# A 17-tap convolution by nested products, woven into a graph network: a bank reassigned, a zero tap dropped, and three asks moved

## The chip, the cores and the metric

The kernel runs on one core of a Trainium2 chip. A core has a matrix engine (TensorE, called PE in the profile, with its weight loads listed as PEld), a vector engine (VectorE, DVE), an activation engine (ScalarE, ACT), a general engine (GpSimd, POOL) and a queue engine (SyncE, SP). Each runs its own stream of instructions in the order in which it was written, and they wait for one another by semaphores. TensorE writes its results to PSUM, a small memory of eight banks of 2 KB per partition; everything else works in SBUF, and transfers to and from the device's main memory are issued on queues by SyncE, GpSimd or ScalarE. The metric is the time of one execution in microseconds (us) of device time, as a median over runs.

## The reference

The input `x` has 32 batches of 512 nodes with 256 channels, and `adj` is one 512 x 512 mask of zeros and ones per batch. All is fp32. Cut to what matters, it computes

```python
h0 = relu(layernorm(x))                              # per node
c  = relu(bn1(conv1x1(h0.T)))
c  = bn2(conv1d(c, conv2_w, 17 taps, pad 8))
x_conv = relu(c + h0.T).T
s  = h0 @ w_se.T + b_se                              # 3 values per node
A  = exp(-dist(s, s)) * adj
x_nmp  = A @ relu(h0 @ w_msg.T + b_msg)
gi = concat(x_conv, x_nmp) @ w_ih.T + b_ih           # GRU cell
gh = h0 @ w_hh.T + b_hh
r, z = sigmoid(gi_r + gh_r), sigmoid(gi_z + gh_z)
out = x + (1 - z) * tanh(gi_n + r * gh_n) + z * h0
```

## The kernel before

**Five streams of work.** The kernel is written as five Python generators: `rows` (normalised rows of the first batches, and the 1x1 convolution `conv1` of all), `begins` (normalise and turn a batch, and store it to `hd` in main memory), `graphs` (messages, exponents, mask, gather), `conv` (the 17-tap convolution) and `gates` (the GRU cell, and the store of the result). A loop at the end of the kernel (`while streams`) takes one step at a time of the stream that is most behind its share. A number `now` stands for TensorE's time and is advanced by every matmul written; a step can say that it is not ready before a certain `now`. Work of the other engines is written by `fill`, which empties a list `LATER` of things due by now (`later(t, f)`), evacuates finished convolution results, and writes operand sums for VectorE (`background`). All of that is decided when the program is built: on the chip there are five fixed instruction streams.

**`settle()`** writes everything that is in `LATER` at once, whatever its due time. It is called in `reset` of the gates, in `graph`, at the second result of each five in the convolution's sums (`summed`), and at the end of each half of the gates.

**The convolution.** The 928 columns of all batches (29 units of 18 outputs each, 32 batches) are cut into seven groups at `STARTS`. Its 17 taps are padded to 18 = 3 x 3 x 2, the first of them zero (line 262), and worked by two nested levels of a three-tap scheme with five evaluation points each, so that a group takes 25 products (`n` from 0 to 24, in the order `ORDER` of points, outer `j1`, inner `j2`). Each product is itself a two-tap convolution. In group 0 it is written out as 16 matmuls. In groups 1 to 6 it takes 12: the sum of both weights (`w[:, 2]`) times the second half of the operand into bank 0 of the PSUM tile `ps_c`; ScalarE copies bank 0 onto bank 1; then each weight times a difference of operand halves (`xd`, made by `ends` on VectorE) is added to its bank. Weights are loaded again from main memory (`wd`) for each product, and `third_weight` makes the sum of both in group 1. The results of five products are combined by VectorE into `z`, and these into `y` (9 values per column); ScalarE also writes the first `y` of a group by three scaled copies of `z`.

**Evacuation.** When a group's `y` is complete, `EVAC` lists its batches, and `evacuate` writes each (bn2 on ScalarE into `part`, then a store to `cd` by GpSimd). Product `n == 4` of the next group waits until `EVAC` is empty (line 774).

**The exponents.** `kernel_exp` takes four PSUM banks for the four 128 x 512 pieces of a batch's distance matrix: three from the pool `ps_g` and a fourth, `extra`, which from group 1 on is bank 0 of a tile `ps_c`, the same pool of one buffer (`cps`) as the convolution's. `bank_at` is set so that the next product is not written before ScalarE has read that bank (lines 789 and 885).

**Rows.** A batch from the eighth on is turned by a detour through main memory: GpSimd stores its rows to `xd`, SyncE loads them back in blocks into `x_sb` (line 943 by `blocks`), VectorE transposes them into `hT`, GpSimd stores that to `hd` (line 954), and SyncE loads it again where it is wanted: `hT` for `conv1` (line 210), `hTg` for the graph and `hTb` for the gates. `load_row` is followed by a delay of 8 in `now`.

**Gates.** A batch's gates read `hTb`, the convolution's result `xconv` (loaded from `cd` by `load_conv`, line 230, added to `hTb` and put through a relu by `residual`), and the gathered sums `xnb`. A result is stored by GpSimd in four pieces (`store`), and the residual input of the next batch, `res`, is loaded by SyncE (`load_res`) into one of two buffers. Its load has to wait until the store has left the buffer. It is asked at `later(now + 5.0, ...)` behind the store (line 1103).

SyncE's queue holds, in one order, the loads of weights, masks, rows, sums, residuals and convolution results. A load that waits holds up all that stand behind it.

Of the kernel before, what the change touches and what calls it, by code (L numbers as in the profile page):

```python
# [32 lines left out]
U = 29  # L33
Q = 18

STARTS = (0, 116, 251, 386, 522, 657, 792, 928)
NG = len(STARTS) - 1
UG = max(j - i for i, j in zip(STARTS, STARTS[1:]))
PER = (STARTS[-1] - STARTS[1]) / (NG - 1) / U
TURNED = 8  # L40
LEAD = 9


ORDER = (3, 0, 4, 2, 1)
# [4 lines left out]
def kernel(  # L49
# [515 lines left out]
    def weights_again(m):  # L565

        w = new_w()
        k = 2 if m < 50 else 3
        nc.sync.dma_start(w[:, :k], WD[m % 25][:, :k])
        WS.append(w)  # L570
        W_AT.append(now + 7.0)

    thirds = set()

    def third_weight(m):
        if m in thirds:
            return
        thirds.add(m)
        w = WS[m]
        dve.tensor_tensor(w[:, 2], w[:, 0], w[:, 1], op=ALU.add)  # L580
        later(dve.free + 0.4, lambda: nc.gpsimd.dma_start(WD[m % 25][:, 2], w[:, 2]))
        W_AT[m] = dve.free + LAG
# [12 lines left out]
    def summed(g):  # L595

        nonlocal read
        y = None  # L600
        _, nh, nz, _ = sizes(g)

        def columns(name, **more):
            return cv.tile([P, NZ], F32, name=name, **more)[:, :nz]

        def add(dst, a, b, op=ALU.add):
            SUMS.append((sums_at, lambda: dve.tensor_tensor(dst, a, b, op=op)))

        def copy(dst, src, scale):
            SUMS.append((sums_at, lambda: later(  # L610
                dve.free + 0.1, lambda: act.activation(dst, src, AF.Copy, scale=scale)
            )))

        def more(dst, a, k, b, op=ALU.add):
            SUMS.append((
                sums_at, lambda: dve.scalar_tensor_tensor(dst, a, k, b, op0=ALU.mult, op1=op)
            ))

        def both(dst, ps):

            nonlocal bank_at, sums_at
            act.activation(dst.rearrange("p (h n) -> p h n", h=2), ps, AF.Copy)
            bank_at = sums_at = act.free + LAG

        for j1 in ORDER:
            got = yield
            sum_all(read)
            n3 = columns("n", bufs=2)
            both(n3, got)
            got = yield  # L630
            sum_all()
            settle()
            z = cv.tile([P, 3 * NZ], F32, name="z")[:, : 3 * nz].rearrange("p (e n) -> p e n", e=3)
            zends = z[:, 0:3:2, :]
            both(z[:, 0, :], got)
            add(z[:, 0, :], z[:, 0, :], n3)
            got = yield
            both(z[:, 2, :], got)
            more(z[:, 2, :], n3, 4.0, z[:, 2, :])
            got = yield  # L640
            n2 = columns("n", bufs=2)
            both(n2, got)
            got = yield
            n1 = z[:, 1, :]
            both(n1, got)
            add(n2, n1, n2, ALU.subtract)
            more(n1, n1, 2.0, n2, ALU.subtract)
            add(zends, zends, n1[:, None, :].to_broadcast([P, 2, nz]))
            more(z[:, 1, :], n3, 2.0, n2)
            read = summed_to + len(SUMS)  # L650
            if j1 == 3:
                y = cv.tile([P, 9 * NZ], F32, name="y")[:, : 9 * nz].rearrange("p (e f n) -> p e f n", e=3, f=3)
                copy(y[:, :, 0], z, 1.0)
                copy(y[:, :, 1], z, 2.0)
                copy(y[:, :, 2], z, 4.0)
            elif j1 in (0, 4):
                add(y[:, :, j1 // 2], y[:, :, j1 // 2], z)
            else:
                for f in range(3):
                    add(y[:, :, f], y[:, :, f], z, ALU.subtract if (f, j1) == (1, 2) else ALU.add)  # L660
        SUMS.append((sums_at, lambda: EVAC.extend(
            (dve.free + 0.3, y, g, b, o) for b in batches(g) for o in range(ND)
        )))
        yield
# [33 lines left out]
    X2, X_AT, XD = [], [], {}  # L698
    at_product = 0
    wide = in_product = exp_waits = False  # L700
    freed, made, made_at, bank_at = -1, 0, 0.0, 0.0

    def all_operands():
# [28 lines left out]

    def convolution():

        nonlocal at_product, cps, wide, in_product

        def product(ps, *terms, clear=(True, True)):

# [22 lines left out]

        for g in range(NG):
            sums = summed(g)
            next(sums)
            nu, nh, nz, rv = sizes(g)
            if g == 1:
                first_ctx.close()
                cps = ctx.enter_context(tc.tile_pool(name="cps2", bufs=1, space=PSUM))
                ps = cps.tile([P, 2, N], F32, name="ps_c")
                matmul(ps[:, 1, :NH], ident, h1[:, :NH], start=True, stop=True)  # L770
                wide = True
            for n in range(25):
                at_product = m = 25 * g + n
                if n == 4:
                    yield lambda: not EVAC
                while 25 <= len(WS) < min(m + 3, 25 * NG):
                    weights_again(len(WS))
                if m == 24:
                    yield lambda: len(WS) >= 25
                if late is None and len(WS) >= 25:  # L780
                    late_pools()
                yield lambda: len(X2) > m and len(WS) > m
                if 25 <= m + 1 < 50 and W_AT[m + 1] <= now:
                    third_weight(m + 1)
                for k in (m, m + 1):
                    if 25 <= k < len(X2) and k not in XD:
                        XD[k] = ends(X2[k], sizes(k // 25)[3])
                        X_AT[k] = dve.free + LAG
                yield max(X_AT[m], W_AT[m], bank_at if g > 0 else 0.0)
                if exp_waits:  # L790
                    yield lambda: not exp_waits
                    yield bank_at
                if 25 <= m < 50:
                    third_weight(m)
                    yield W_AT[m]
                w, x2 = WS[m], X2[m]
                if g == 0:
                    ps = cps.tile([P, N], F32, name="ps_c")[:, :nz]
                    d0, d1, d2 = (x2[:, 0, :], 0), (x2[:, 1, :], 0), (x2[:, 0, :], 1)
                    product(ps[:, :nh], (0, *d0), (1, *d1))  # L800
                    hand()
                    yield now
                    product(ps[:, nh:], (0, *d1), (1, *d2))
                else:
                    in_product = True
                    ps = cps.tile([P, 2, N], F32, name="ps_c")[:, :, :nh]
                    product(ps[:, 0, :], (2, x2[:, 1, :], 0), clear=(True, False))
                    act.activation(ps[:, 1, :], ps[:, 0, :], AF.Copy)
                    yield act.free + LAG
                    for k in range(2):  # L810
                        product(ps[:, k, :], (k, XD[m][:, k, :], 0), clear=(False, False))
                    del XD[m]
                WS[m] = X2[m] = None
                done = ps if g > 0 else ps.rearrange("p (h n) -> p h n", h=2)
                if g > 0:
                    later(now + 0.3, hand)
                at_product = m + 1
                yield now
                if g > 0:
                    yield lambda: done is None  # L820
            hand()
# [44 lines left out]
    def kernel_exp(at):  # L866

        nonlocal now, bank_at, exp_waits
        exp_waits = False
        if not wide:  # L870
            extra = acc.tile([P, N], F32, name="ps_acc")
        else:
            extra = cps.tile([P, 2, N], F32, name="ps_c")[:, 0, :]
        pss = [extra, bank(), bank(), bank()]
        for c in range(NT):
            k = slice(32 * c, 32 * c + 5)
            nc.tensor.matmul(  # L877
                pss[c], gr.left[k, :], gr.right[k, :], start=True, stop=True,
                tile_position=(32 * c, 0),
            )  # L880
        now += 1.15
        for c in range(NT):
            act.activation(at[:, c, :], pss[c], AF.Exp)
            if c == 0:
                bank_at = act.free + LAG

    def masked(b, at, c):

# [130 lines left out]
    def gates(b):  # L1019
# [73 lines left out]
        def store(y, o, s):  # L1093
# [6 lines left out]
                )  # L1100
            if s.stop == N:
                del XR[b, o]
                later(now + 5.0, lambda: load_res(b + 1, o))

        for o in range(ND):
            r = z = None
# [104 lines left out]
    turn_of = 0  # L1211

    def sum_some():
        if not SUMS or SUMS[0][0] > max(now, dve.free) + 0.1:
            return False
        sum_all(summed_to + 1)
        return True
# [7 lines left out]
    def background():  # L1225
# [9 lines left out]
        if sum_some():  # L1235
            return True
        for m in range(max(25, at_product), min(len(WS), 50)):
            if m not in thirds and W_AT[m] <= now:
                third_weight(m)
                return True  # L1240
        for _ in range(3):
# [177 lines left out]
```

## Time and profile before

| what | value |
|---|---|
| median of 5 runs | 2117.6 us (2111.85 to 2118.55) |
| the profiled execution | 2111.85 us, span 2110.0 us |
| TensorE busy | 2055.1 us (97%) |
| VectorE, ScalarE, GpSimd busy | 1368.8, 814.9, 339.4 us |
| matmul records of `ps_c<-xd,w` and `ps_c<-x,w` | 2400 and 2000 |
| TensorE's waits for `hT<-hd`, for `xconv`, for the exponents | 12.8, 7.4 and 6.7 us |
| SyncE's wait for stores of `out_dram<-res` | 471.3 us in 102 waits |

The profile is of one execution; its own time, 2111.85 us, is the time to hold against its rows, and the median is another matter. An fp32 matmul leaves two records in it, so 2400 records are 1200 matmuls. A record's mean duration is not what a matmul costs, since they overlap; the cost is the distance from one to the next in a run without waits. In the list of waits, a line gives the engine and what it was about to write, what it waited for, the total in us, how often, and the longest. In a timeline, a line gives the start, the length of a run of like instructions, and in brackets how long the engine stood still before it, and for what. A helper records most operations, so that L126 (vector and activation) and L135 (matmuls) are lines of helpers, and tiles tell the work apart.

### The profile page before, as it was taken

How to read it: one execution, taken by the hardware profiler on the slowest of the kernel's cores; microseconds unless marked ns; L12 is line 12 of the kernel's file. 1: busy time of each engine (PE TensorE's matmuls, PEld its weight loads, DVE VectorE, ACT ScalarE, POOL GpSimd, SP SyncE). 2: the span in 40 equal slices, each digit the busy share in tenths (PEclk: the TensorE clock that was granted, in tenths of full speed). 3: DMA queues.
4: the chain of work that ended last, by engine and by line, in shares of the span. 5: the costliest groups of instructions: out<-in, count | busy, mean ns of one | idle time of the engine just before them, and what ended most of it. 6: DMA issues, size and time to landing. Idle time of an engine off the chain costs nothing.

```text
span 2110.0 us, 25907 instructions
## 1 busy us (share of the span) xinstructions
PE 2055.1 (97%) x8764; PEld 1260.1 (60%) x8764; DVE 1368.8 (65%) x2448; ACT 814.9 (39%) x1431; POOL 339.4 (16%) x582
## 2 busy tenths in 40 slices
PE   9999899999999999999999999999999989999998
PEld 5887665656566655666556665456665556654444
DVE  6887677877677485786567772667763846654323
ACT  5544453344433344333354333434333432224121
POOL 2001121121211112111121110211111111012111
PEclk9999999999999999999999999999999999999999
DMA  7456798676777777766586766775767455734342
GB/s 287 161 185 193 242 261 225 174 230 181 216 188 201 205 193 203 194 168 226 145 222 187 205 200 173 186 187 162 206 179 199 143 153 135 199 111 117 85 95 40
DMA packets 546436, 383.07 MB, mean 182 GB/s; under 512 B 456576, under 2 KB 473472, under 8 KB 545664
## 3 DMA queue, kind: packets, MB, share of 16 engines
q1 hardware_dynamic: 512992, 282.17, 50.0%
q0 software_dynamic: 28624, 86.01, 13.3%
q10 hardware_dynamic: 4688, 13.24, 1.7%
q8 instruction: 70, 1.15, 0.2%
q14 instruction: 62, 0.51, 0.1%
HBM read 281.95 MB, written 99.35 MB: 181 GB/s over the span
## 4 chain that ended last, share of the span: by engine, by line
PE 78%; issue 10%; DVE 5%; DMA 3%; ACT 2%; POOL 2%; SPq 1%; POOLq 0%; DVEq 0%; ACTq 0%
PE ps_acc L135 39%; PE ps_c L135 20%; PE ps_g L135 16%; PE ps_g L140 1%; DVE x L126 1%; DMA w<-wd 1%; PE ps_c L877 1%; POOL out_dram L1097 1%; DMA hT<-hd 1%; DVE z L126 1%; DVE xd L126 0%; SPq L338 0%; PE ps_acc L145 0%; DVE st L126 0%; DVE at L126 0%
## 5 line engine op out<-in xcount | busy, mean ns | idle before, releaser
L135 PE MATMUL ps_acc<-xconv,wih 128*128 128x512 f32 (+1 forms) x772 | 363.7, 594 | 7.4 <-ACT xconv L126 7.4
L135 PE MATMUL ps_acc<-xnb,wih 128*128 128x512 f32 (+1 forms) x772 | 361.1, 593 | 0.0
L135 PE MATMUL ps_acc<-hTb,whh 128*128 128x512 f32 (+1 forms) x772 | 355.6, 590 | 0.0
L135 PEld LDWEIGHTS ps_c<-xd,w 128*128 128x128 f32 x2400 | 299.1, 190 | 72.3 <-issue 61.5
L135 PEld LDWEIGHTS ps_c<-x,w 128*128 128x128 f32 x2000 | 253.4, 192 | 90.9 <-issue 63.7
L135 PE MATMUL ps_c<-xd,w 128*128 128x135 f32 (+1 forms) x2400 | 302.0, 278 | 2.8 <-ACT ps_c L126 2.7
L135 PE MATMUL ps_c<-x,w 128*128 128x135 f32 (+2 forms) x2000 | 260.9, 279 | 14.1 <-ACT at L126 6.7
L1097 POOL DMA_DIRECT2D out_dram<-res x252 | 164.0, 657 | 629.5 <-DVE res L126 551.8
L135 PEld LDWEIGHTS ps_acc<-xconv,wih 128*128 128x128 f32 x772 | 141.1, 190 | 150.8 <-issue 140.3
L135 PE MATMUL ps_g<-at,msg 128*128 128x512 f32 x512 | 227.7, 596 | 0.6 <-DVE at L126 0.5
L135 PEld LDWEIGHTS ps_acc<-xnb,wih 128*128 128x128 f32 x772 | 141.1, 191 | 138.7 <-issue 136.0
L135 PEld LDWEIGHTS ps_acc<-hTb,whh 128*128 128x128 f32 x772 | 140.5, 190 | 139.6 <-issue 137.2
L126 DVE TENSOR_TENSOR msg<-ps_g,bmsg 128x256 f32<-128x256 f32 x128 | 53.6, 420 | 190.4 <-PE ps_g L135 190.3
L135 PEld LDWEIGHTS ps_g<-at,msg 128*128 128x128 f32 x512 | 95.6, 191 | 110.1 <-issue 105.0
L126 DVE TENSOR_TENSOR o_sb<-hTb,r 128x512 f32<-128x512 f32 x63 | 43.4, 689 | 172.8 <-ACT r L126 172.6
L126 DVE SCALAR_TENSOR_TENSOR x<-x,x 128x544 f32<-128x544 f32 (+5 forms) x161 | 137.6, 855 | 2.8
L126 ACT ACTIVATE ps_c<-ps_c 128x270 f32<-128x270 f32 (+1 forms) x150 | 58.0, 386 | 197.5 <-PE ps_c L135 197.4
L126 DVE TENSOR_TENSOR xd<-x 128x544 f32<-128x544 f32 (+1 forms) x150 | 106.9, 717 | 40.2 <-PE ps_c L135 40.0
L135 PE MATMUL ps_g<-hT,w 128*128 128x512 f32 (+4 forms) x288 | 119.2, 561 | 13.0 <-DMA hT<-hd 12.8
L126 DVE TENSOR_TENSOR x<-x 128x272 f32<-128x272 f32 (+5 forms) x280 | 126.8, 497 | 0.2
L135 PE MATMUL ps_g<-wmsg,hTg 128*128 128x259 f32 x496 | 123.8, 382 | 0.1
L126 ACT ACTIVATE h<-ps_g,bn_shift,bn_scale 128x252 f32<-128x252 f32 (+4 forms) x208 | 85.6, 485 | 70.8 <-PE ps_g L135 70.7
(124 smaller groups left out, 2274.7 us busy)
## 6 DMA issues: line engine op xcount, KB each, us to landing
w<-wd SPq DMA_DIRECT2D x125, 768.0 KB, 5.1
m_sb<-in_adj_dram SPq DMA_DIRECT2D x384, 64.0 KB, 3.3
hd<-hT POOLq DMA_DIRECT2D x32, 512.0 KB, 5.6
hT<-hd SPq DMA_DIRECT2D x32, 512.0 KB, 4.4
hTb<-hd SPq DMA_DIRECT2D x32, 512.0 KB, 5.6
xnb<-nd SPq DMA_DIRECT2D x64, 256.0 KB, 3.4
xconv<-cd SPq DMA_DIRECT2D x32, 512.0 KB, 6.3
res<-in_x_dram SPq DMA_DIRECT2D x256, 64.0 KB, 2.5
```

The costliest lines, as they stand in the source:

```text
L126: getattr(self.engine, name)(*tiles, **more)
L135: nc.tensor.matmul(ps, lhsT, rhs, **more)
L140: nc.tensor.transpose(ps, a, ident)
L877: nc.tensor.matmul(pss[c], gr.left[k, :], gr.right[k, :], start=True, stop=True, tile_position=(32 * c, 0),)
L1097: queue.dma_start(OB[b][:, s.start // 32 : s.stop // 32, o * P + 32 * g : o * P + 32 * g + 32], y[at, s].rearrange("i (k j) -> i k j", j=32),)
```

## The change

It has five parts.

- The exponent's fourth bank is bank 1 of one lasting tile `pair`, which the convolution uses for all products from group 1 on; `bank_at` is no longer set by the exponents.
- The hold for the evacuation moves from product 4 to product 6, and the three copies that begin a group's `y` wait, as an entry without a time in `SUMS`, until `EVAC` is empty. `y` is allocated there.
- Where both evaluation points are 0 (`n == LONE == 6`), the first weight is the zero tap. Its products are left out: in group 0 the two that use it, and in the other groups the product becomes two direct ones with `w[:, 1]`, without the third weight, the copy and the differences. The load of its weights shrinks with it.
- The residual is asked at `now + 12` instead of `now + 5`.
- The groups' edges move by one column in places.

```diff
-STARTS = (0, 116, 251, 386, 522, 657, 792, 928)
+STARTS = (0, 116, 252, 388, 523, 658, 793, 928)
+LONE = 6
@@ weights_again
-        k = 2 if m < 50 else 3
-        nc.sync.dma_start(w[:, :k], WD[m % 25][:, :k])
+        k = slice(1, 2) if m % 25 == LONE else slice(0, 2 if m < 50 else 3)
+        nc.sync.dma_start(w[:, k], WD[m % 25][:, k])
@@ third_weight
-        if m in thirds:
+        if m in thirds or m % 25 == LONE:
@@ summed
-                copy(y[:, :, 0], z, 1.0)
-                copy(y[:, :, 1], z, 2.0)
-                copy(y[:, :, 2], z, 4.0)
+                def first(z=z):
+                    nonlocal y
+                    y = cv.tile([P, 9 * NZ], F32, name="y")...
+                    for f in range(3):
+                        later(dve.free + 0.1, lambda f=f: act.activation(
+                            y[:, :, f], z, AF.Copy, scale=float(1 << f)
+                        ))
+                SUMS.append((None, first))
@@ convolution
-                ps = cps.tile([P, 2, N], F32, name="ps_c")
-                matmul(ps[:, 1, :NH], ident, h1[:, :NH], start=True, stop=True)
+                pair = cps.tile([P, 2, N], F32, name="ps_c")
+                matmul(pair[:, 1, :NH], ident, h1[:, :NH], start=True, stop=True)
-                if n == 4:
+                if n == 6:
                     yield lambda: not EVAC
-                    product(ps[:, :nh], (0, *d0), (1, *d1))
+                    product(ps[:, :nh], *[(0, *d0)][n == LONE :], (1, *d1))
-                    product(ps[:, nh:], (0, *d1), (1, *d2))
+                    product(ps[:, nh:], *[(0, *d1)][n == LONE :], (1, *d2))
-                    ps = cps.tile([P, 2, N], F32, name="ps_c")[:, :, :nh]
-                    product(ps[:, 0, :], (2, x2[:, 1, :], 0), clear=(True, False))
-                    act.activation(ps[:, 1, :], ps[:, 0, :], AF.Copy)
-                    yield act.free + LAG
-                    for k in range(2):
-                        product(ps[:, k, :], (k, XD[m][:, k, :], 0), clear=(False, False))
+                    ps = pair[:, :, :nh]
+                    if n == LONE:
+                        for k in range(2):
+                            product(ps[:, k, :], (1, x2[:, 1 - k, :], k), clear=(True, False))
+                    else:
...

@@ kernel_exp
-            extra = cps.tile([P, 2, N], F32, name="ps_c")[:, 0, :]
+            extra = pair[:, 1, :]
-            if c == 0:
-                bank_at = act.free + LAG
@@ store
-                later(now + 5.0, lambda: load_res(b + 1, o))
+                later(now + 12.0, lambda: load_res(b + 1, o))
@@ sum_some
-        if not SUMS or SUMS[0][0] > max(now, dve.free) + 0.1:
+        if not SUMS:
+            return False
+        if EVAC if SUMS[0][0] is None else SUMS[0][0] > max(now, dve.free) + 0.1:
             return False
```

## The prediction

> **What bounds the kernel now.** I read the head of the page, the waits of TensorE, the timeline of TensorE where it stands still, and then the queue lines behind its longest stop.
>
> ```profile
> span 2110.0 us, 25907 instructions
> PE 2055.1 (97%) x8764; PEld 1260.1 (60%) x8764; DVE 1368.8 (65%) x2448; ACT 814.9 (39%) x1431; POOL 339.4 (16%) x582
> ...
> PE 78%; issue 10%; DVE 5%; DMA 3%; ACT 2%; POOL 2%; SPq 1%; POOLq 0%; DVEq 0%; ACTq 0%
> ```
>
> TensorE is busy for 97% of the span; the next engine, VectorE, for 65%. So an edit counts only by what it does to TensorE's own work (2055.1 us) or to its stops (the other 55 us, some of them at the start and the end). Its waits, in total, times and longest:
>
> ```profile
> PE ps_g L135 <- DMA hT<-hd: 12.8, 6, 7.8
> PE ps_acc L135 <- ACT xconv L126: 7.4, 1, 7.4
> PE ps_c L135 <- ACT at L126: 6.7, 10, 0.7
> PE ps_c L135 <- DVE x L126: 3.5, 1, 3.5
> ...
> SPq L919 <- DMA out_dram<-res: 471.3, 102, 27.1
> ```
>
> The first three are the ones that this change touches: a batch's rows that come back late from `hd`, one late `xconv`, and ten short waits for the exponents. SyncE's queue waits 471.3 us for stores of results before it may load residuals; TensorE feels that only through loads that stand behind them. The stops on TensorE's timeline:
>
> ```profile
> 331.66 1.07 PE L135 MATMUL ps_c<-x,w 128*128 128x135 f32 x7 [0.67 <-ACT at L126]
> 1375.16 1.76 PE L135 MATMUL ps_g<-hT,w 128*128 128x171 f32 x5 [7.76 <-DMA hT<-hd]
> 1702.26 1.22 PE L135 MATMUL ps_acc<-xconv,wih 128*128 128x512 f32 x1 [7.37 <-ACT xconv L126]
> ```
>
> A long stop costs more than its length. The windows of TensorE around both (busy time, instructions, granted clock, DMA share, GB/s) show half clock:
>
> ```profile
> 1371.00:1375.00 4.00, 0.00 (x0) 0.50 0.90 288
> 1375.16:1380.77 5.61, 5.61 (x13) 0.53 0.29 64
> ...
> 1702.26:1708.45 6.19, 6.19 (x14) 0.52 0.04 13
> ```
>
> In windows of 1 us the clock falls to half about 3 us after TensorE stopped, and stays there 10.2 us; of that 5.3 and 5.9 us are work at half speed, so 2.7 and 2.9 us are lost on top of the stops. The chain behind the stop at 1375, from the SyncE and GpSimd queues:
>
> ```profile
> 1344.36 2.61 POOL L1097 DMA_DIRECT2D out_dram<-res  x4 [5.04 <-DVE right L126]
> ...
> 1363.13 0.54 POOL L954 DMA_DIRECT2D hd<-hT  x1 [6.83 <-DVE hT L126]
> ```
> ```profile
> 1349.00 1.97 SPq L919 DMA_DIRECT2D res<-in_x_dram  x4
> 1351.07 2.34 SPq L338 DMA_DIRECT2D m_sb<-in_adj_dram  x4
> 1353.51 4.52 SPq L919 DMA_DIRECT2D x_sb<-xd  x8
> ...
> 1368.66 0.32 SPq L210 DMA_DIRECT2D hT<-hd  x1
> ```
>
> Batch 27's turned input is loaded at 1353.51, transposed, stored to `hd` at 1363.13, loaded back at 1368.66 and used at 1375.16: 21.65 us. The written order puts 20.6 us of TensorE work between that first load and its use, and the load ran 6.9 us behind its place because the residual's load ahead of it waited for the store. 21.65 - 20.6 + 6.9 = 7.95; the stop is 7.76. This sum I use below.
>
> **The change, part by part.**
>
> *Zero tap.* Two pieces of the chain that ended last (start, length), of conv matmuls alone, at 116 and at 135 columns:
>
> ```profile
> 50.00 10.71 PE ps_c L135 x96
> ...
> 456.11 1.84 PE ps_c L135 x16
> ```
>
> A matmul leaves two records, so they are 48 and 8 matmuls: 0.223 and 0.230 us each. Six groups lose 4 of 12 matmuls, the first 8 of 16: 24 x 0.230 + 8 x 0.223 = **-7.3**, all on TensorE. The dropped differences, copies and weight loads lie beside it: nothing.
>
> *Group edges.* The groups' columns sum to 928 as before. Edge 523 instead of 522 gives group 3 one column of batch 18: one more row of 4 matmuls (27 columns wide, no row so narrow; between 0 and the 0.223 above): **+0.9**, and one more load.
>
> *Exponent's bank.* Line 873 took a tile whose hold (line 789, `bank_at`) kept the next product away until the exponent was read. Now both are slices of one tile `pair`, and the hold is gone. In the compiled order the first matmul of the product behind the exponents still waits for the first exponent's ACTIVATE in 25 of 26 places. The program's dependency is the tile's, not the bank's. The product now stands directly behind the exponents in 18 places, before in 11, of which ten show 0.67. 18 x 10/11 x 0.67 = 11.0 against 6.7: **+4.3**. Ends: -6.7 if the wait vanished, +10 if all 25 stood still. Queued behind the waiting matmul is all of TensorE's stream.
>
> The Trainium skill, "PSUM — Partial Sum Buffer", summary of rules for kernel authors, advises matmuls into a different bank than the one being read. By it the wait would vanish and the sum be 11 us lower; the waits written in the program speak against, and no run here shows it yet.
>
> *Two more products before evacuation.* The hold at n == 4 is now at n == 6, and the copies into `y` wait until EVAC is empty. TensorE shows no wait at that place now, since other streams fill it. A product is 12 x 0.23 = 2.8 us; bounds -2.8 to +2.8 (a late `y` copy), and I take **0**: ScalarE, busy 39%, covers it. If not, the next `z` sum is late.
>
> *Residuals later.* `later(now + 12)` instead of 5. But `settle()` in `reset` and in `graph` empties the list long before. In the written order the residual's load still stands directly behind its store: 1.2 us of TensorE work apart on average before, 0.7 after. So this part does nothing by itself: **0**, and the 471 us stay. Ends: 0 and the shift of loads below.
>
> *What moves with it: rows loaded straight behind their own store.* Before at batches 22 and 27, after at 18, 22, 26, 27, 31. TensorE work from the `xd` load to the use, in that order: 22.4, 26.0, 24.1, 20.6, 23.4 us. With the 21.65 above, slack at 18, 22, 26, 31 is 0.75, 4.35, 2.45, 1.75 us. At 26 a residual stands 2.6 us ahead of the load; loads with one just ahead ran 3.4 to 6.9 us late before (batches 27 to 30), so 5 - 2.45 = 2.5 us (0 to 7). At 31 it stands 10 us ahead: 1 (0 to 5); at 18 none: 0.5. Batch 27's queue order is as before: 7.8. The small ones of before (batches 24, 26, 30: 5.1 in all) have moved; I keep 2. Sum 13.8 against 12.8: **+1.0** (-5 to +10). Half clock after the stop at 26: three stretches of 3.4 us at half follow short stops (from 233, 257 and 465 us), 1.7 us lost each; half of one, **+0.8** (0 to 2.7).
>
> *`xconv` of batch 22.* Its store asks stand 16.5 us of TensorE work ahead of the use instead of 13.8: 7.4 - 2.7 = 4.7, **-2.7** (-7.4 to 0). Half clock then starts 3 us into it: if it lasts 10.2 us again, 8.5 of them are work and 4.3 are lost instead of 2.9 (+1.4); if 3.4 us, 0.9 are lost (-2.0). I take **-0.5**. The waits not named, each under 3.6 us, I leave as they are.
>
> The Trainium skill, "TensorE: Matmul & The Clock Gate", part 1, has the clock back after about one busy window of 3.4 us; the rows here show 5.3 and 5.9 us of work at half clock. By the page this stop's loss would be 1.7 us at most.
>
> Sum: -7.3 + 0.9 + 4.3 + 0 + 0 + 1.0 + 0.8 - 2.7 - 0.5 = **-3.5 us**. The profiled execution took 2111.85 us, 1.85 of it outside the span, and is the lowest of five; the median, 2117.6, lies 5.75 higher. So 2108.3 for an execution like the profiled one, **2114** for the median.
>
> **Rivals.**
> - *The bank works as named.* -4.3 - 6.7 more: 2103. For: two banks. Against: the waits in the program. 0.07.
> - *Slower: rows come back late.* If one of the new chains stands like batch 27's (7.8 + 2.7 = 10.5 instead of 3.3 at batch 26), the sum is +3.7: 2121; with two of them about +14: 2132. It decides once a load runs 7 us or more behind its place. For: batch 27's did, and 26 has the same order, a residual behind a fresh store. Against: batches 28 to 30 were 3.4 to 4.6 late. 0.22.
> - *`xconv` stays late.* The load waits for the same store of a residual, and the stop moves along with it: -3.5 + 2.7 + 0.5 = -0.3, 2117.3. 0.18.
> - *Batch 27 comes free*, as earlier work shifts its queues: -10.5 more, 2103.5. Its order is unchanged, so 0.08.
>
> **How the numbers follow.** Forecast 0.45. About 0.2% (4.2 us) is what a measurement can tell from no change, and the forecast lies just inside that line: of its 0.45, 0.20 is faster, 0.22 within, 0.03 slower. First and last rival: 0.15 faster. `xconv`: 0.04 faster, 0.11 within, 0.03 slower. Late rows: 0.05 within, 0.17 slower. Sums: faster 0.39, same 0.38, slower 0.23. The range 2101 to 2127 leaves out the case of two full stops and the lower end of the first and last rivals, under 0.2. The forecast's own range is 2108 to 2120, about half of the way to the ends of its terms.
>
> **What would show it.** In the changed kernel's profile: 2304 records of `ps_c<-xd,w` instead of 2400, TensorE busy some 6 us less; waits of `ps_c` for the exponents some 16 times 0.67; SyncE's wait for `out_dram<-res` near 470; a stop of 7 to 8 us at batch 27's rows and small ones at 18, 26 and 31; `xconv` near 4.7. Wrong would make it: exponent waits gone, or a second stop over 7 us with a half-clock stretch behind it.

## The result

The changed kernel takes 2116.41 us (median of 32 runs, 2112.25 to 2123.28) against 2115.84 us before (55 runs, 2110.47 to 2122.51): ratio 1.0005, 95% interval 0.9999 to 1.0011. That is no change. The prediction was 2114 us, 3.5 us below the kernel before, with most of its chance split between a little faster and no difference.

The head of the page of the changed kernel, and TensorE's and SyncE's waits (total, times, longest):

```profile
span 2116.5 us, 25837 instructions
PE 2058.0 (97%) x8714; PEld 1263.1 (60%) x8714; DVE 1366.7 (65%) x2441; ACT 815.4 (39%) x1431; POOL 337.7 (16%) x582
...
PE 84%; issue 8%; DVE 3%; DMA 2%; ACT 1%; POOL 1%; SPq 0%; POOLq 0%; ACTq 0%; DVEq 0%
```
```profile
PE ps_c L136 <- ACT at L127: 15.1, 18, 3.2
PE ps_g L136 <- DMA hT<-hd: 9.8, 3, 5.1
PE ps_c L136 <- ACT n L127: 9.1, 3, 3.7
PE ps_c L136 <- ACT z L127: 3.8, 2, 2.3
...
PE ps_acc L136 <- ACT xconv L127: 2.3, 1, 2.3
...
SPq L929 <- DMA out_dram<-res: 473.5, 104, 19.5
```

By the prediction's count TensorE was given 7.3 us less to do for the zero tap, and it was busy longer: 2058.0 us instead of 2055.1. The reason is the clock. I divided both spans into windows of 1 us and summed busy time times the missing part of the granted clock: 10.5 us before (5 stretches), 20.9 after (12 stretches). At full speed the work is then 2055.1 - 10.5 = 2044.6 us before and 2058.0 - 20.9 = 2037.1 after, 7.5 less. Such a figure is good to some 2 us: the kernel before with nothing but a third residual buffer, the same matmuls in the same order, gives 2042.9. So the two profiled executions differ like this: work -7.5, time without a matmul +3.5 (55.0 to 58.5), lost to half clock +10.4; together +6.4 of the +6.5 us between the spans.

The pair exaggerates the clock. Before, the profiled execution had a mean granted clock of 0.992, but the mean of 23 executions is 0.9899; after, 0.989 in the profile and 0.9885 in the mean of 33. In the means the missing clock, counted over the whole span with its stops, is 0.0101 x 2116 = 21.4 us and 0.0115 x 2117 = 24.3 us, a lasting difference of about 3 us. With 3 in place of 10.4 the three parts come to about -1 us, beside +0.6 between the medians. Single executions of one kernel differ by 10 us, and the slower ones mostly have the lower clock.

The stops of the changed kernel that matter, on TensorE's timeline (start, length of the run of instructions, idle time ahead of it and what ended it):

```profile
282.05 1.20 PE L136 MATMUL ps_c<-x,w 128*128 128x136 f32 x8 [3.04 <-ACT n L127]
...
300.90 3.58 PE L136 MATMUL ps_c<-x,w 128*128 128x136 f32 x16 [3.66 <-ACT n L127]
...
357.17 1.20 PE L136 MATMUL ps_c<-x,w 128*128 128x136 f32 x8 [0.67 <-ACT at L127]
...
1315.64 6.37 PE L136 MATMUL ps_g<-hT,w 128*128 128x512 f32 x8 [4.16 <-DMA hT<-hd]
1389.44 2.86 PE L136 MATMUL ps_g<-hT,w 128*128 128x189 f32 x8 [5.10 <-DMA hT<-hd]
1460.51 3.50 PE L136 MATMUL ps_c<-x,w 128*128 128x135 f32 x16 [3.22 <-ACT at L127]
...
1716.41 3.21 PE L136 MATMUL ps_acc<-xconv,wih 128*128 128x512 f32 x4 [2.28 <-ACT xconv L127]
```

Four things are to be seen. The wait behind the exponents is there as often as the compiled order said, 18 times: 16 times it is 0.67 us, once 1.17 and once 3.22. Two new stops of over 3 us stand where group 0 is being evacuated. Batches 26 and 27 wait for their rows. And `xconv` is late by 2.28 instead of 7.37.

The first of the two new stops is the evacuation's. ScalarE's timeline (the changed kernel, same columns):

```profile
280.19 1.35 ACT L127 ACTIVATE part<-y,bn_shift,bn_scale 128x522 f32<-128x522 f32 x1 [1.68 <-DMA cd<-part]
281.33 0.66 ACT L127 ACTIVATE n<-ps_c 128x544 f32<-128x544 f32 x1
...
300.22 0.62 ACT L127 ACTIVATE n<-ps_c 128x544 f32<-128x544 f32 x1 [4.43 <-DVE z L127]
```

With the hold two products later, a product is written while `part` is still being emptied. Its copy out of PSUM (`n<-ps_c`) stands in ScalarE's order behind an evacuation that waits for a store of `cd`, and the next product on TensorE waits for that copy. The second stop is the copy of a later result, which waits for VectorE to finish with `z`; why VectorE is late there is not shown. Each is followed by a stretch at half clock: the windows behind them read (busy, clock, DMA share, GB/s)

```profile
283.00:286.40 3.40, 3.40 (x8) 0.56 1.11 292
300.90:304.30 3.40, 3.40 (x16) 0.56 0.82 277
```

The long wait for an exponent has another cause on the same engine:

```profile
1455.03 0.61 ACT L127 ACTIVATE n<-ps_c 128x540 f32<-128x540 f32 x1
1455.53 4.44 ACT L127 ACTIVATE y<-z 128x1620 f32<-128x1620 f32 x3
1459.86 0.59 ACT L127 ACTIVATE at<-ps_c 128x512 f32<-128x512 f32 x1
```

Three copies that begin a group's `y` (4.44 us) stand ahead of the exponent, so the wait for the tile is 3.22 us instead of 0.67.

### The profile page after: what moved, and what is told of

Read it like the earlier page. It is cut to its first block, busy times and chain, and to the rows that moved or that the text cites. A ratio compares the mean times of both kernels' runs of the same rounds, so it can differ in the third digit from the quotient of the medians.

```text
span 2116.5 us, 25837 instructions
## 1 busy us (share of the span) xinstructions
PE 2058.0 (97%) x8714; PEld 1263.1 (60%) x8714; DVE 1366.7 (65%) x2441; ACT 815.4 (39%) x1431; POOL 337.7 (16%) x582
## 4 chain that ended last, share of the span: by engine, by line
PE 84%; issue 8%; DVE 3%; DMA 2%; ACT 1%; POOL 1%; SPq 0%; POOLq 0%; ACTq 0%; DVEq 0%
PE ps_acc L136 42%; PE ps_c L136 22%; PE ps_g L136 17%; PE ps_g L141 1%; PE ps_c L889 1%; ACT at L127 1%; DMA hd<-hT 1%; POOL out_dram L1107 0%; PE ps_acc L146 0%; DMA hT<-hd 0%; DMA cd<-part 0%; DVE st L127 0%; DVE z L127 0%; DMA m_sb<-in_adj_dram 0%; PE ps_g L889 0%
## 5 line engine op out<-in xcount | busy, mean ns | idle before, releaser
L136 PEld LDWEIGHTS ps_c<-xd,w 128*128 128x128 f32 x2304 | 287.7, 190 | 67.5 <-issue 58.7
L136 PEld LDWEIGHTS ps_c<-x,w 128*128 128x128 f32 x2032 | 260.0, 194 | 109.3 <-issue 57.0
L136 PE MATMUL ps_c<-x,w 128*128 128x135 f32 (+2 forms) x2032 | 269.3, 282 | 31.3 <-ACT at L127 15.1
L136 PE MATMUL ps_c<-xd,w 128*128 128x135 f32 (+1 forms) x2304 | 289.8, 278 | 1.1 <-ACT ps_c L127 1.1
L136 PE MATMUL ps_g<-hT,w 128*128 128x512 f32 (+8 forms) x296 | 120.7, 558 | 9.8 <-DMA hT<-hd 9.8
L127 ACT ACTIVATE h<-ps_g,bn_shift,bn_scale 128x252 f32<-128x252 f32 (+8 forms) x212 | 86.6, 483 | 88.2 <-PE ps_g L136 88.0
```

The costliest lines, as they stand in the source:

```text
L127: getattr(self.engine, name)(*tiles, **more)
L136: nc.tensor.matmul(ps, lhsT, rhs, **more)
```

## The experiments

Each kernel was timed beside runs of the kernel before on the same chip; the ratios are to those. The last four ran on another chip than the first eight, and the kernel before had medians from 2115.7 to 2117.8 us in the three sessions, so experiments of different sessions are compared by ratio. My theory was: the exponents' wait belongs to the tile, so the change doubles it, and this with the late rows and the clock eats the zero tap's gain. Its rivals: the parts gain or lose by themselves, or only because they shift the order in SyncE's queue behind the residual's wait.

**The zero tap alone.** The kernel before with `LONE` and nothing else.

```diff
+LONE = 6
-                    product(ps[:, 0, :], (2, x2[:, 1, :], 0), clear=(True, False))
+                    if n == LONE:
+                        for k in range(2):
+                            product(ps[:, k, :], (1, x2[:, 1 - k, :], k), clear=(True, False))
+                    else:
+                        product(ps[:, 0, :], (2, x2[:, 1, :], 0), clear=(True, False))
...
```

> The kernel before with the zero tap's products left out and nothing else. If the matmuls' count sets the time: 32 matmuls fewer, -7.3 us of work, the exponents' waits stay at 10 to 11 times 0.67 us, and the time is 2108 to 2110 (before: 2115.8). The rival says that what is saved comes back as stops, because the written order shifts (rows of batches 26 and 31 are now loaded straight behind their store, as in the changed kernel): 2113 to 2117, with longer waits for hT or xconv. A third: the stretches at half clock, 5 in the profile of before and 12 in that of the changed kernel, go with the exponents; then this kernel keeps about 5.

Measured: 2117.76 us against 2117.81, ratio 0.9996 (0.9987 to 1.0006). The gain is absent although no other part of the change is there. The waits say where it went:

```profile
PE ps_c L136 <- ACT at L127: 13.9, 11, 4.6
PE ps_g L136 <- DMA hT<-hd: 9.5, 2, 5.4
PE ps_g L136 <- DVE aug L127: 6.2, 1, 6.2
```

Eleven waits for the exponents instead of ten, but 13.9 us instead of 6.7, since two of them (4.65 and 3.22) stand behind the three `y` copies; a new wait of 6.2 us; and 21.5 us lost to half clock in the profile (10.5 before), with a mean clock of 0.9856 over 11 executions (0.9899 before). The rival's time was right, but not its reason: rows wait 9.5 us instead of 12.8, and `xconv` 0.2 instead of 7.4. The third expectation, about 5 stretches, was wrong: there are 10.

In group 0 the gain turns into a wait on the spot. The kernel before, and behind it this one:

```profile
78.52 3.73 PE L135 MATMUL ps_c<-x,w 128*128 128x116 f32 x32
82.20 0.56 ACT L126 ACTIVATE n<-ps_c 128x464 f32<-128x464 f32 x1 [2.31 <-DVE z L126]
...
78.38 1.94 PE L136 MATMUL ps_c<-x,w 128*128 128x116 f32 x16
82.07 0.56 ACT L127 ACTIVATE n<-ps_c 128x464 f32<-128x464 f32 x1 [2.31 <-DVE z L127]
82.68 3.23 PE L136 MATMUL ps_c<-x,w 128*128 128x116 f32 x16 [2.36 <-ACT n L127]
```

The copy out of PSUM waits for VectorE's `z` and comes at the same time in both. The 8 matmuls that covered that time (1.8 us) are gone, so the next product waits 2.36 us for the copy, and a stretch at half clock follows it (1.7 us lost). The same stop is in the changed kernel, at 84.88.

**The bank alone.** The kernel before with `pair`, the exponent in its second bank, and no hold.

```diff
-            extra = cps.tile([P, 2, N], F32, name="ps_c")[:, 0, :]
+            extra = pair[:, 1, :]
-            if c == 0:
-                bank_at = act.free + LAG
```

> The kernel before with the exponent's bank alone changed: the lasting tile, its second bank for the exponents, no hold behind them. The product now stands directly behind the exponents in 19 of 26 places instead of 11. If the wait is on the tile and not the bank: 18 to 19 waits of 0.67 us, some 13 us in all instead of 6.7, and more stretches at half clock behind them (1.7 us each); 2120 to 2126. If the bank alone decided, the waits would be gone: 2107 to 2110.

Measured: 2132.49 us, ratio 1.0071 (1.0053 to 1.0088). 19 waits for the exponents, 16.7 us in all (6.7 before): 18 of 0.67 and one of 4.64, again behind the `y` copies. The wait is the tile's, as expected. But 15 us is more than the waits cost: rows 16.1 instead of 12.8, `xconv` 8.2 instead of 7.4, and 18.2 us lost to half clock instead of 10.5. Which of these come from the bank itself and which from the shifted order is not separated.

**The hold put back.** The changed kernel, with the two lines for `bank_at` restored.

```diff
             act.activation(at[:, c, :], pss[c], AF.Exp)
+            if c == 0:
+                bank_at = act.free + LAG
```

> The changed kernel with the hold behind the exponents put back (bank_at set by the exponents as before). The product stands directly behind the exponents in 7 places instead of 18. If the exponents' waits and their half-clock stretches are where the zero tap's gain went: waits of some 5 us instead of 15, fewer stretches, 2104 to 2109 (changed kernel: 2116.4). If not, the time stays within 2114 to 2118.

Measured: 2123.53 us, ratio 1.0031 (1.0021 to 1.0041). That is a miss: by the ratios some 5.5 us slower than the changed kernel (1.0005). The exponents' waits fell as meant, from 15.1 to 7.2 us in 7 places, but `xconv` waits rose from 2.3 to 11.2, rows from 9.8 to 12.4, and a new wait for `aug` took 3.1. So a hold that saves 8 us of one wait can lose more than it saves in other waits, since the order of everything else moves with it.

**The banks as two tiles.** The changed kernel; the reads of the exponents then hold up only the second bank. Results are copied out in two ScalarE instructions.

```diff
-                pair = cps.tile([P, 2, N], F32, name="ps_c")
+                pair = [cps.tile([P, N], F32, name=f"ps_c{k}") for k in "ab"]
...
-            extra = pair[:, 1, :]
+            extra = pair[1]
...
+                for h in range(2):
+                    act.activation(halves[:, h, :], ps[h], AF.Copy)
```

> The changed kernel with the lasting tile split into two tiles of one bank each, so that the exponents' reads hold up only the second bank; results are copied out by two ScalarE instructions instead of one (some 150 more of about 0.25 us). If the wait was the tile's: no wait for the exponents directly behind them, -12 to -15 us, and fewer stretches at half clock, 2098 to 2104. Rival: the wait moves to the second bank's copy behind the four exponents on ScalarE, or to ScalarE as a whole, and the time is 2112 to 2118.

Measured: 2100.23 us, ratio 0.9921 (0.9903 to 0.9939), 16 us less than the changed kernel's 2116.41. The wait for the exponents shrinks to one of 2.2 us:

```profile
PE ps_g L136 <- DMA hT<-hd: 8.3, 3, 4.8
PE ps_cb L894 <- ACT z L127: 5.5, 2, 4.0
PE ps_cb L894 <- ACT n L127: 3.9, 1, 3.9
PE ps_ca L136 <- DVE x L127: 3.4, 1, 3.4
PE ps_ca L136 <- ACT ps_cb L127: 2.9, 4, 1.3
PE ps_c L136 <- ACT n L127: 2.4, 1, 2.4
PE ps_cb L136 <- ACT at L127: 2.2, 1, 2.2
```

The first three are now rows, and exponents that wait until the last result has left their bank. TensorE's time without a matmul falls from 58.5 to 43.7 us, of which the exponents' waits are 12.9, and the loss at half clock from 20.9 to 16.9. So the two banks do what the change's words say only when the program's dependency is kept by bank too.

**Three residual buffers in the kernel before.** The written order stays the same on all five engines; only what the residual's load waits for is older.

```diff
-            XR[b, o] = late.tile([P, N], F32, name="res", bufs=2)
+            XR[b, o] = late.tile([P, N], F32, name="res", bufs=3)
```

> The kernel before with three buffers for the residual instead of two, so that its load no longer waits for the store just issued; the written order is the same on every engine. If the residual's wait on SyncE's queue is what makes rows and convolution results late: SyncE's wait for out_dram<-res falls from 471 us to under 50, the stops at batch 27's rows (7.8 us) and at xconv (7.4 us) shrink to under 2, their half-clock stretches go, and the time falls by 12 to 20 us, to 2098 to 2105. If the rows are late of themselves (store, load, turn), the stops stay and the time is within 2114 to 2118.

Measured: 2096.80 us, ratio 0.9900 (0.9884 to 0.9916). SyncE's queue around batch 27's rows, the stretch that the prediction showed of before:

```profile
1345.15 1.96 SPq L919 DMA_DIRECT2D res<-in_x_dram  x4
1347.21 2.08 SPq L338 DMA_DIRECT2D m_sb<-in_adj_dram  x4
1349.40 4.69 SPq L919 DMA_DIRECT2D x_sb<-xd  x8
...
1364.51 0.32 SPq L210 DMA_DIRECT2D hT<-hd  x1
```
```profile
SPq L919 <- DMA out_dram<-res: 38.7, 21, 6.7
```
```profile
PE ps_g L135 <- DMA hT<-hd: 1.0, 1, 1.0
```

SyncE's wait for the stores is 38.7 us instead of 471.3, the load of batch 27's turned input is issued 1.0 us behind its place in the written order instead of 6.9, and of 12.8 us of waits for rows 1.0 is left. `xconv` still waits 4.9 of its 7.4 us: there the store of `cd` itself is late (its load went at 1680.95, 0.4 us after SyncE had come to it, held by `cd<-part`, which GpSimd had issued at 1676.67), so I was wrong that it would go too. The time without a matmul falls from 55.0 to 38.5 us. One line is worth 1% here, and no wait of TensorE names it.

**The changed kernel with both cures.** The two edits above together: two tiles, three buffers.

> The changed kernel with the two banks as tiles of their own and three residual buffers. The stops left in it for hT (8.3 us) and xconv (1.8 us), with two stretches at half clock (4.7 us), should go if the residual's wait made them: 8 to 14 us below the two-bank kernel, 2087 to 2092. If not: 2097 to 2103.

Measured: 2089.04 us, ratio 0.9865 (0.9847 to 0.9883), the fastest kernel of this study. Rows wait 2.2 us once.

**The residual asked at 5.** One number in the changed kernel.

```diff
-                later(now + 12.0, lambda: load_res(b + 1, o))
+                later(now + 5.0, lambda: load_res(b + 1, o))
```

> The changed kernel with the residual asked at 5 instead of 12. The written order is the same on every engine but for a few lines of SyncE's queue, so nothing should move: 2114 to 2119 (changed kernel: 2116.4). The rival, that the later ask keeps the queue free, would have it slower, above 2121.

Measured: 2119.43 us, ratio 1.0010 (0.9997 to 1.0022), beside the changed kernel's 1.0005. The part has no measurable effect, as the written order said: `settle()` empties the list before the delay runs out.

**The evacuation's hold back at product 4.**

```diff
-                if n == 6:
+                if n == 4:
```

> The changed kernel with the evacuation's hold back at product 4 (the copies that begin a group's sums still wait for the end of the evacuation). No wait on TensorE names the hold, so its own worth is within 3 us; but the order shifts, and the product stands directly behind the exponents in 22 places instead of 18 and batch 26's rows are no longer loaded straight behind their store. Waits for the exponents some 3 us more, a stop at batch 27 of 3 to 6 us: 2114 to 2122. If the two more products were a gain of their own (the sums' waits for n and z, 9.1 and 3.8 us, grow without them), 2124 or more.

Measured: 2125.62 us, ratio 1.0038 (1.0024 to 1.0052). The waits for `n` fall from 9.1 to 2.9 us and those for `z` from 3.8 to 2.6, so 7.4 us of waits go with the two more products; the second alternative's time came out, but its reason, that these waits grow, is wrong. The first of the two stops shows it best. ScalarE and TensorE at the same place:

```profile
279.28 1.34 ACT L127 ACTIVATE part<-y,bn_shift,bn_scale 128x522 f32<-128x522 f32 x1 [1.56 <-DMA cd<-part]
280.42 0.66 ACT L127 ACTIVATE n<-ps_c 128x544 f32<-128x544 f32 x1
```
```profile
275.26 7.03 PE L136 MATMUL ps_g<-at,msg 128*128 128x512 f32 x16
282.13 3.66 PE L136 MATMUL ps_g<-wmsg,hTg 128*128 128x259 f32 x16
285.63 1.09 PE L136 MATMUL ps_c<-x,w 128*128 128x136 f32 x8
```

The copy stands behind the evacuation here too, but with the product held back TensorE has gather and message matmuls until 285.63, and it does not wait. The kernel is slower all the same: 21 waits for the exponents with 17.6 us, new or longer waits for `aug`, `h` and `at` of 10 us together, and 24.0 us lost to half clock. I can't say which of these belong to the hold and which to the shift of order.

**Parts of the change with three buffers.** These four ask what the parts are worth when the residual no longer decides; all have the line `bufs=3` of above. The first is the changed kernel with that line.

> The changed kernel, in its own order, with three residual buffers. Compared with the kernel before with three (2096.8) it shows what the change is worth when the residual's wait no longer decides. By the terms: matmuls -7.5, exponents' waits 15.1 instead of 6.7 (+8.4), the sums' waits of the evacuation part some +6, a few stretches at half clock: 2098 to 2106. If the residual's wait had hidden a gain of the change, 2088 to 2093.

Measured: 2103.26 us, ratio 0.9942 (0.9926 to 0.9959). Against the kernel before with the same cure (0.9900, on the other chip) the change costs 0.4%. The profiled executions say the same: work -7.0 us, time without a matmul +11.4 (38.5 to 49.8), lost to half clock +3.0. What the change gained on late rows and `xconv` counts for little once the queue no longer makes them late, and its own waits remain.

```profile
PE ps_c L136 <- ACT at L127: 15.1, 18, 3.2
PE ps_c L136 <- ACT n L127: 8.9, 3, 3.7
PE ps_c L136 <- ACT z L127: 3.7, 2, 2.3
```

They are the same three lines as in the changed kernel with two buffers, to 0.2 us.

The second is the kernel before with the zero tap left out, in the same written order as the run without the third buffer.

> The kernel before with the zero tap's products left out and three residual buffers. With two it gained nothing (2117.8 against 2117.8). If that gain had gone into stops behind the residual's wait, it now appears: 2087 to 2092 (2096.8 - 7.3 = 2089.5). If it goes into waits that have nothing to do with the queue (the exponents' 4.6 and the 6.2 us for aug seen in that kernel, with their stretches at half clock): 2094 to 2098.

Measured: 2102.82 us, ratio 0.9942 (0.9925 to 0.9959). A miss on both sides: the zero tap's 32 matmuls are gone, and the kernel is not faster than without that part (0.9900). SyncE's wait for the stores is down to 38.4 us, so the lost gain does not lie in the queue. The profiled execution (2098.08 us) beside that of the kernel before with three buffers (2097.38) shows where it goes: work -7.1 us, time without a matmul +9.1 (38.5 to 47.6), lost to half clock -1.6. Of the 9.1, the exponents' waits are 7.1 (13.8 instead of 6.7, with 4.64 and 3.22 behind the `y` copies) and the copy in group 0 is 2.4. The medians lie further apart than these two executions, with a mean clock of 0.9892 against 0.9932 (some 8 us). One trace can't say where that part is lost, and the two ran on different chips.

The third is the kernel before with the bank's part alone.

> The kernel before with the exponent's bank alone changed and three residual buffers. With two it lost 15 us, of which the waits for the exponents were 10. Without the queue's part: +8 to +13, 2105 to 2110. If the bank alone cost nothing and all was the shifted queue: 2095 to 2099.

Measured: 2110.72 us, ratio 0.9973 (0.9960 to 0.9986), 0.7% above the kernel before with three buffers, again on the other chip: the bank alone costs about 15 us with or without the queue's help. The waits for the exponents are again 16.7 us (+10.0); the rest goes with the clock, 0.9908 against 0.9932, which is 5 us, though the profiled executions do not show that part (half clock costs 14.0 and 14.1 us in them).

The fourth is the kernel before with the zero tap left out and the banks as two tiles.

> The kernel before with three parts only: zero tap left out, the two banks as tiles of their own, three residual buffers; edges, evacuation's hold and the residual's ask as before. By the terms: 2096.8 - 7.3 - 6.7 (no wait for the exponents) + some 2 for the second bank's copy: 2084 to 2088. If the evacuation's hold and edges of the change are worth something here, it stays above the changed kernel with both cures, 2089.0.

Measured: 2097.94 us, ratio 0.9910 (0.9891 to 0.9930), with executions from 2090.35 to 2100.31. A miss: I had expected 2084 to 2088, and by the ratio it is no faster than the kernel before with three buffers (0.9900). Its profiled execution was its fastest, 7 us below that kernel's: work -7.6, time without a matmul +2.0, lost to half clock -1.7, with 5.2 us of waits for the exponents in two places. So in the trace the zero tap's gain is there once those waits are mostly gone. Over all six executions it is not: the mean clock is 0.9907 against 0.9932, some 5 us, for a reason that stays open. It stays above the kernel with all parts and both cures (0.9865), which ran on another chip; that the edges and the evacuation's hold are worth something there is possible and not shown.

## Why the prediction was right, and where it was not

The time came out inside the range and 2.4 us above its number, but the small gain of 3.5 us is not there: the medians differ by +0.6 us, with an interval from -0.2 to +2.3. Two main readings held: the zero tap's matmuls are real work that goes, and the exponents' wait stays with the tile. What I had not seen is that the zero tap's gain is lost even without the bank's part. Of the signs that I named, 2304 records of `ps_c<-xd,w`, 18 waits and SyncE's 473.5 us came; TensorE's busy time rose instead of falling. That the sum came so close is in part luck: the waits for exponents, `n` and `z` and the clock were priced too low, and rows, `xconv` and waits that I had left as they are came out shorter.

- *Zero tap and edges* (-7.3 + 0.9 = -6.4): the work at full clock fell by 7.5, close to that. But "all on TensorE, nothing beside it" was wrong in group 0, where 1.8 us of the gain became a wait of 2.36 us with a half-clock stretch behind it.
- *Exponent's bank* (+4.3): mis-sized. It measured +8.4 (15.1 against 6.7). The 18 places were right, but all 18 stood still, not ten in eleven, and two of them for longer (1.17 and 3.22). I had priced each at 0.67 without asking what stands ahead of the exponent on ScalarE; for the longer one it was three `y` copies.
- *Two more products before evacuation* (0, bounds -2.8 to +2.8): this step failed. I named the cover, ScalarE at 39%, and it wasn't there: ScalarE works in order, and one instruction that waits 1.68 us for a store of `cd` holds up the copy out of PSUM behind it, for which TensorE stood 3.04 us. The waits for `n` and `z` rose from 4.0 to 12.9 us, of which 2.36 is the zero tap's in group 0; with the hold back at product 4 they fell to 5.5.
- *Residuals later* (0): right; the run at 5 showed it.
- *Rows* (+1.0): measured -3.0. The way to work it out held: at batch 26 the load stood 9.8 us behind its place and the chain took 18.71 us, 18.71 - 24.1 + 9.8 = 4.4 against a stop of 4.16; at batch 27 19.57 - 20.6 + 6.4 = 5.4 against 5.10. What I had wrong was taking 7.8 for batch 27 again and 21.65 for the chain; both came out shorter.
- *`xconv`* (-2.7): -5.1, the right sign.
- *Half clock* (+0.8 - 0.5): +10.4 in the two profiles and about +3 in the mean of many executions. I priced stretches only behind stops for rows and `xconv`, and each of the other stops of over 2 us in the changed kernel has one too. My bound of 1.7 us for a stop's loss was also too low: work at half clock can begin in the middle of one step of 3.41 us and last through the next (see the last section), as the 5.3 and 5.9 us behind the two long stops show.

The rival that the bank works as named was wrong for this kernel and right for the split one, at -16 us where I had said -11 (the exponents' waits alone fell by 12.9). The rival of late rows did not come true, but its cause, the residual's wait on SyncE's queue, was worth more than all parts of the change: 20 us in the kernel before. I quoted its 471 us, said that TensorE feels them only through what stands behind, and did not add up what that is.

The Trainium skill's advice in "PSUM — Partial Sum Buffer", summary of rules for kernel authors, to aim at a different bank than the one being read and to guard by bank, is borne out by the split kernel (no wait of 0.67 us left). The changed kernel followed only its first half: the program's dependency was by tile, and 18 waits stayed.

## What to carry to other kernels

Where two uses share a tile, moving one to another bank took no wait away here until the tile itself was split: read the waits that the compiled program holds, not the addresses. A queue's wait that no engine seems to feel (471 us here) is still worth asking who stands behind it; one more buffer can be the cheapest edit in the kernel. And in an order that a planner writes, removing work shifts everything else: time the part alone before you credit it, and look for instructions that now stand behind something slow on an in-order engine.

## What I had not expected of the hardware

Stretches of 3.4 us at half clock can follow stops as short as 2.2 to 3 us, and cost up to 1.7 us each on top (stops of 2.26 and 2.83 us of before had none). They can also follow the exponents, whose matmuls use 5 of 128 rows, when only a third of a microsecond of waiting is added. In the changed kernel:

```profile
751.09 0.69 PE L889 MATMUL ps_c<-right,left 5*128 5x512 f32 x1
...
752.52 1.12 PE L889 MATMUL ps_g<-right,left 5*128 5x512 f32 x2 [0.29 <-ACT h L127]
753.57 2.92 PE L136 MATMUL ps_acc<-xconv,wih 128*128 128x512 f32 x4
756.28 1.06 PE L136 MATMUL ps_acc<-xnb,wih 128*128 128x512 f32 x1
```

Four matmuls of `xconv` take 2.92 us there instead of 1.88, and the windows of 1 us show the clock at half from 754 to 757. TensorE had stood for 0.29 us only. The same stretch, behind the same operations and about 0.3 us of wait, is in the kernel before (from 465 us), with the zero tap alone (745) and with the bank alone (470). So these matmuls of few rows seem to count as little activity.

The traces of all fourteen runs bear that out. In each, the half-clock stretches begin on one grid with steps of 3.413 us (to 4 ns) and, but for the one behind the last matmul, last one, two or three steps. I took every step at full clock and added its time without a matmul to its time with nothing but 5-row matmuls. Where that comes to 2.14 us or more, half clock follows, in 107 of 107 steps; below, it follows in 11 of 8337, none of them under 1.79 us. If 5-row matmuls count as work the line is lost: 21 stretches then follow a step with less than 1 us of standstill. So it matters where a stop falls. Of the 2.83 us only 2.01 lay in one step; the usual 0.67 us behind the exponents, with 1.07 us of their matmuls, comes to 1.74; and the stop of 3.22 us was followed by one step at half clock in the changed kernel and by two with the zero tap alone. This is read from traces; no run was made to try it.
